# Second batch of a causal attention: tiles 8-9 by seven half-size products, tiles 6-7 with both scores in one step, and a new order of tiles and block loads

## The chip, the core and the metric

The kernel runs on one core of a Trainium2 chip. The engines named here are TensorE (PE, with its weight loads as PEld), VectorE (DVE), ScalarE (ACT), GpSimd (POOL) and the queue that SyncE feeds with transfers (SP). The metric is the device time of one launch in microseconds (us), the median of three runs.

## What is computed

The input x has 2 batches of 2048 tokens of 512 features. The part of the reference that matters here, shortened:

```python
xn = _layernorm(x)
q, k, v = x_norm @ qkv          # x_norm: xn normalised again
scores = einsum('bsk,btk->bst', q, k) * scale
scores = where(causal, scores, -inf)
attn = softmax(scores)
s = (attn @ v) @ o_proj + xn
g = silu(mixture_of_8_experts(xn, top 2))
return x + s * g
```

All of it is float32. The experts' result is stored in DRAM before the attention starts, and the attention gathers its rows back, two for each token.

## The kernel before

The attention is the last stage, about the last 400 us of the launch. It works on tiles of 128 queries, 16 in each batch, 32 in all; a list `seq` (L1014) gives their order. A place in that list is called a slot here: slots 0 to 15 are tiles 15 down to 0 of the first batch, slots 16 to 31 are tiles of the second batch. A causal tile t looks at keys 0 to 128(t+1)-1, in blocks of 512 keys; so tile 8 has two whole blocks and 128 keys more, tile 6 one block and 384 keys. Two slots that stand together share a query load and make a pair; pair 8 is slots 16 and 17, pair 9 is slots 18 and 19.

One long loop `for s in range(NT + OUT + 2)` (L1760) emits the program. In step s it emits scores of slot s, row maxima, exponentials, their transposition, and the product with the values of an earlier slot. Every engine works through its own instructions in exactly that order; nothing reorders them. The pieces, with the lines that the profile shows:

- Scores. `chunk_scores` (L1307 on PE) makes the scores of one slot against one key block with four matmuls into a PSUM bank. DVE masks the diagonal (L1312) and takes a maximum (L1295); `end_scores` joins the maxima to `nm` (L1395).
- Scores by seven products. For the pairs in `SCORED`, `fast_scores` makes the scores of both slots against the first two key blocks with seven products of half depth (L1359), 14 matmuls of 512 columns where the direct form takes 16. It needs sums of query parts, `query_sums` (L1326 to L1329, DVE, one step earlier), and sums of key parts, `block_sums` (L1340, the tile `tk`, one for each batch). ACT copies the first product out of PSUM (L1378), and DVE adds the others into place (L1365).
- Exponentials. `exponentials` runs on ACT (L1485). For slots with more than three tiles of keys POOL splits each result into halves (L1495), SP issues a transposing DMA (L1501), and DVE joins the halves again (`join_p`, L1517). Slots with up to three tiles of keys are turned by PE (L1512) and copied back by ACT (L1513).
- Values. `values` multiplies one slot directly (L1535, matmuls of 512 columns). For the pairs in `FAST` seven half-size products do it (L1583 and some of L1535, 256 columns each): `combine_p` makes sums of the two slots' probabilities (L1577, DVE), `combine_v` sums of the value blocks (L1557, tiles `vT`), and `values_first`, `values_next` and `values_end` make the products `p12`, `p57`, `p64` and `p03`. ACT copies a part of `p12` (L1611), and DVE adds up (L1600).
- Output. `gate` prepares the gathered rows (ACT L1688, DVE L1689, ACT L1691), `attended` scales the result (ACT L1696, DVE L1699), and `emit` finishes it on POOL (L1707, L1708). In an ordinary step, `attended` of an older slot comes on DVE ahead of the masks and maxima of the step.

[...] a pool "a" of five (scores, transposed tiles, products of the scores) and a pool "b" of three (products with values). Blocks of keys and values of the second batch are loaded during the first batch, by a table `parts_b` of steps; `later` is a table of the steps in which DVE makes `block_sums` and `combine_v` for the second batch. `joins` holds the `join_p` of the slot before.

Of the kernel before, what the change touches and what calls it, by code (L numbers as in the profile page):

```python
# [26 lines left out]
def gated_attention_moe(  # L27
# [32 lines left out]
    NT = B * S // P  # L60
    BT = 4
    TB = BT * P
    NB = NT // BT
    NBB = S // TB
# [928 lines left out]
    def fetch(store, pool, src, name, tag):  # L993

        def part(b, c):
            if c == 0:
                store[b] = pool().tile([P, src[b].shape[1], src[b].shape[2]], F32, name=f"{name}_{b}", tag=tag)
            nc.sync.dma_start(out=store[b][:, c, :], in_=src[b][:, c, :])
        return part
# [12 lines left out]

    assert B == 2 and NBB == 4
    seq = [t for t in reversed(range(NBB * BT))]  # L1014
    seq += [NBB * BT + t for t in (8, 9, 0, 1, 6, 7, 2, 3, 4, 5, 10, 11, 12, 13, 14, 15)]
    assert all(seq[s] // 2 == seq[s + 1] // 2 for s in range(0, NT, 2))
    fetch_k = fetch(aks, lambda: kp2, kt_d, "k2", "kT")
    fetch_v = fetch(avs, lambda: vp, v_d, "v2", "v")
# [249 lines left out]
    OUT = 4  # L1268


    SCORED = (0, 1, 2, 3, 13, 14, 15)
    FAST = SCORED + (4,)

    def place(s):
        b, t = divmod(seq[s], BT)
        return b, t, b - b % NBB
# [21 lines left out]
    def direct(s):  # L1298

        return range(2 if s // 2 in SCORED else 0, len(widths[s]))  # L1300

    def chunk_scores(s, j):
        b, t, first = place(s)
        w = widths[s][j]
        ps = ps_a.tile([P, TB], F32, name=f"ps_{s}_{j}", tag="a")
        for c in range(ND):
            nc.tensor.matmul(  # L1307
                ps[:, :w], lhsT=aqs[seq[s] // 2][:, c, ts(t % 2, P)], rhs=aks[first + j][:, c, :w],
                start=(c == 0), stop=(c == ND - 1),
            )  # L1310
        if first + j == b:
            nc.vector.tensor_tensor(ps[:, w - P : w], ps[:, w - P : w], keep, ALU.min)  # L1312
        maximum(s, ps[:, :w], j * TB)
# [79 lines left out]
    def end_scores(s):  # L1393
        mx, nm, pieces = scored[s]
        nc.vector.tensor_reduce(nm, mx[:, : len(pieces)], AX.X, ALU.max, negate=True)  # L1395
# [23 lines left out]
    for i in range(NM):  # L1419
# [21 lines left out]
        for _ in range(3):  # L1441
            if i >= paired.stop and early:
                f, b, c = early.pop(0)
# [249 lines left out]
    def attended(s):  # L1693
        n = seq[s]
        o = outs[s] if s // 2 in FAST else op.tile([P, D], F32, name=f"o_{s}", tag="o", bufs=4)
        nc.scalar.activation(  # L1696
# [34 lines left out]
    def emit_ahead(s, o, cols, attention=None):  # L1731
# [6 lines left out]

    K = NBB
    parts_b = [(0, fetch_v, 0), (0, fetch_v, 1), (0, fetch_v, 2), (0, fetch_v, 3),  # L1740
               (4, fetch_k, K + 2), (6, fetch_v, K + 2), (8, fetch_k, K + 1), (10, fetch_v, K + 1),
               (12, fetch_k, K), (14, fetch_v, K), (20, fetch_k, K + 3), (22, fetch_v, K + 3)]
    parts_b = [(s, f, b, c) for s, f, b in parts_b for c in range(ND)]
    parts_b.sort(key=lambda part: part[0])

    later = {}
    for steps, f, b in (
        ((10, 10, 11, 11), combine_v, K + 2), ((12, 12, 13, 13), combine_v, K + 1),
        ((20, 21, 22, 23), block_sums, K), ((24, 25, 26, 27), combine_v, K),
    ):  # L1750
        for i, step in enumerate(steps):
            later.setdefault(step, []).append((f, b, (i + 1,)))
# [6 lines left out]

    for s in range(NT + OUT + 2):  # L1760
        fast = s // 2 - 1 in FAST
        pair = (s, s + 1) if s // 2 in SCORED else (s,)
        if s < NT and (s % 2 == 0 or len(pair) == 1):
            for k in pair:
                if s:
                    begin_scores(k)
                room(k)
        n = s // 2 + 1
        if s % 2 == 0 and NQ <= n < NT // 2:
            for c in range(2):  # L1770
                fetch_q(n, c)
        if s == 0:
            fetch_parts(s, NBB * ND)
            block_sums(0)
        late = []
        for k in range(NT):
            if k not in AHEAD:
                wait = 4 - k % 2 if k // 2 in FAST else 3
                if s == k + wait:
                    late.append((attended, k))  # L1780
                if s == k + wait + 1:
                    emit(k)
        if s == NT:

            values_first(s - 2)
            for k in AHEAD:
                make_ahead(k)
        if len(pair) == 1 or s % 2:
            for f, *args in late:
                f(*args)  # L1790
        for k in range(NT):
            if s == (NT - 1 if k in AHEAD else k + 2 - k % 2 if k // 2 in FAST else k + 1):
                fetch_inputs(k)
        if s == NT - 1:
            gather_y(NT - 2)
        if s % 2 and s > 3 and s // 2 + 1 in SCORED:
            query_sums(s + 1, nc.vector)
        joins = []
        for k in () if s == 1 else (0, 1) if s == 2 else (s - 1,):
            if 0 <= k < NT - 1 and not by_te(k):  # L1800
                joins += [(join_p, k)] * len(halves[k])
        chunks = []
        if s < NT and s != 1:
            chunks = [(k, j) for k in ((1,) if s == 0 else (s,)) for j in direct(k)]
        if s == 0:

            for k, j in chunks:
                chunk_scores(k, j)
            chunks = []
        if s < NT and s % 2 == 0 and len(pair) == 2:  # L1810
            pools = [(ps_a, "a")] * 5 + [(ps_b, "b"), (ps_a, "a")]
            if s < 3:
                pools = [(ps_b, "b")] * 3 + [(ps_a, "a")]
            if s == 2:
                joins = [(combine_v, b, (1,)) for b in range(NBB - 1)] + joins
            now = 5 if s == 2 else 1
            fast_scores(s, pools, late + joins[:now])
            joins = joins[now:]
            if s == 0:
                query_sums(2, nc.gpsimd)  # L1820
        for k, j in chunks:
            chunk_scores(k, j)
            if s != 3 and joins:
                f, *args = joins.pop(0)
                f(*args)
        if s != 3:
            for f, *args in joins:
                f(*args)
        if 0 <= s - 1 < NT and by_te(s - 1):

            if not fast:
                values(s - 2)
            turn_p(s - 1)
        if s < NT and s != 1:
            end_scores(s)
        if fast and s % 2 == 0 and 2 < s < NT:
            combine_p(s - 2)
        if 0 <= s - 1 < NT:
            divisor(s - 1)
        if s < NT:  # L1840
            if s != 1:
                exponentials(s)
            if s % 2 == 0 and len(pair) == 2:
                maximum(s + 1, turned[s + 1][:, : 2 * TB], 0)
            if s == 0:
                end_scores(1)
                exponentials(1)
            fetch_parts(s, 4)
            for f, *args in later.pop(s, []):
                f(*args)  # L1850
        if s == 2:
            pass
        elif s == 3:
            combine_p(0, (1, 3, 2))
            for b in range(NBB - 1):
                combine_v(b, (2,))
            values_first(0)
            combine_p(0, (4,))
            for b in range(NBB - 1):
                combine_v(b, (4,))  # L1860
            values_next(0)
            for f, *args in joins:
                f(*args)
            values_end(0, [lambda: query_sums(s + 1, nc.vector)])
        elif s == NT:
            emit_ahead(s - 2, seven[s - 2][1], LO)
            values_next(s - 2)
        elif fast and s % 2 == 0:
            values_first(s - 2)

            if s != NT - 2:
                values_next(s - 2)
        elif fast and s == NT - 1:
            values_next(s - 3)
            values_end(
                s - 3,
                [lambda: join_p(s)] * len(halves[s])
                + [lambda: combine_p(s - 1, (1, 3)), lambda: gate(s - 1)]
                + [lambda: combine_p(s - 1, (2, 4))],
            )  # L1880
        elif fast:
            values_end(s - 3)
        elif 0 <= s - 2 < NT and not (s - 1 < NT and by_te(s - 1)):
            values(s - 2)

        for k in range(0, NT - 2, 2):
            if s == (k + 2 if k + 2 in AHEAD else k + 3):
                gate(k)
        for k in range(0, NT - 2, 2):
            if s == k + 1:  # L1890
                gather_y(k)
        if s == 1:

            for b in (2, 0, 1):
                combine_v(b, (3,), nc.gpsimd)
# [45 lines left out]
```

## Time and profile before

| | us |
|---|---|
| median of three runs (1007.63, 1008.37, 1008.95) | 1008.37 |
| the profiled execution | 1007.83 |
| its span, from first to last instruction | 1006.0 |
| PE busy, of the span | 999.9 |
| PEld busy | 665.3 |
| DVE busy | 716.9 |
| ACT busy | 403.2 |
| POOL busy | 483.3 |

The span and the profiled time differ by 1.8 us, which lies around the first and last instruction. The busy time of PE is that of matmuls whose records overlap each other; a float32 matmul of the program stands in the trace as two records, so a group of "x8" is four matmuls. Times in the timeline are counted from the start of the span. The stage between slots 16 and 20, which the change touches most, lies between 777 and 815 us in this execution.

### The profile page before, as it was taken

The numbers are of one execution on the slowest core, as the hardware profiler recorded it, in microseconds if no ns is written. First come the engines' busy times: TensorE is split into PE (matmuls) and PEld (weight loads), VectorE is DVE, ScalarE is ACT, GpSimd is POOL, SyncE is SP. The second block draws the span as 40 slices with busy tenths as digits, with TensorE's granted clock in tenths as the row PEclk, the third lists the DMA queues.
The fourth block names the chain that finished last, engine by engine and source line by source line (L and its number), as shares of the span: only waits on it lengthen the run. The fifth ranks groups of instructions, "written<-read, shape, count | busy, mean of one in ns | idle before, by whom it ended". The sixth has DMA issues, their size and how long they took to land. (4 is left out here: it accounts for less than half of the span.)

```text
span 1006.0 us, 13431 instructions
## 1 busy us (share of the span) xinstructions
PE 999.9 (99%) x3924; PEld 665.3 (66%) x3924; DVE 716.9 (71%) x1396; ACT 403.2 (40%) x804; POOL 483.3 (48%) x475
## 2 busy tenths in 40 slices
PE   9999999999999999999999999999999999999998
PEld 5888888874567767766753448677675544447577
DVE  6996746897887777677744579668576556878667
ACT  3344445322444454444445112232335535442241
POOL 4474564004644454444332165254557776764272
PEclk9999999999999999999999999999999999999999
DMA  8689996978999999999999576274677768753361
GB/s 293 193 264 293 329 286 258 349 249 240 202 227 220 211 208 221 217 200 222 216 218 242 164 193 147 78 206 104 183 199 239 225 200 240 207 141 86 92 165 42
DMA packets 296647, 207.96 MB, mean 207 GB/s; under 512 B 230776, under 2 KB 243832, under 8 KB 296576
## 3 DMA queue, kind: packets, MB, share of 16 engines
q1 hardware_dynamic: 282432, 163.56, 63.2%
q0 software_dynamic: 10400, 34.63, 12.5%
q10 hardware_dynamic: 3744, 8.91, 2.4%
q8 instruction: 34, 0.56, 0.2%
q14 instruction: 37, 0.30, 0.1%
HBM read 92.35 MB, written 60.03 MB: 151 GB/s over the span
## 5 line engine op out<-in xcount | busy, mean ns | idle before, releaser
L1195 PE MATMUL py<-arena,ht 128*128 (+3 forms) x396 | 176.7, 593 | 0.0
L1307 PE MATMUL ps<-k,q 128*128 128x512 f32 (+3 forms) x416 | 143.0, 495 | 0.3 <-PEq L1455 0.3
L1495 POOL COPY pu<-pT 128x1024 uint16<-128x1024 uint16 (+2 forms) x74 | 82.5, 1146 | 118.1 <-ACT pT L1485 59.1
L1166 POOL COPY hu<-h 128x704 uint16<-128x704 uint16 x66 | 61.9, 956 | 155.8 <-issue 121.7
L1195 PEld LDWEIGHTS py<-arena,ht 128*128 128x128 f32 (+3 forms) x396 | 71.8, 185 | 80.7 <-issue 76.9
L1307 PEld LDWEIGHTS ps<-k,q 128*128 128x128 f32 x416 | 74.7, 190 | 67.1 <-issue 56.5
L970 POOL DMA_INDIRECT xs<-zu_d,toki x66 | 77.6, 1176 | 70.2 <-DVE toki L791 55.6
L1181 ACT ACTIVATE ht<-ht,b1sel 128x128 f32<-128x128 f32 (+3 forms) x216 | 67.9, 380 | 88.1 <-DVE ht L1175 88.1
L1145 DVE TENSOR_TENSOR h<-p,h 128x176 f32<-128x176 f32 x182 | 55.5, 337 | 60.7 <-PE p L1138 57.2
L1678 POOL DMA_INDIRECT yg<-y_d,posi x64 | 67.4, 1053 | 36.9 <-DVE yg L1689 21.9
L1535 PE MATMUL po<-v,pT 128*128 128x512 f32 x152 | 67.9, 592 | 0.0
L347 POOL COPY zu<-z 128x1024 uint16<-128x1024 uint16 x32 | 39.9, 1245 | 55.7 <-DVE z L332 55.7
L1517 DVE COPY pT<-puT 128x1024 uint16<-128x1024 uint16 (+2 forms) x74 | 54.1, 759 | 8.8 <-DMA puT<-pu 8.6
L1485 ACT ACTIVATE pT<-pT,nm 128x1024 f32<-128x1024 f32 x14 | 16.1, 1148 | 110.3 <-DVE nm L1395 72.0
L1203 ACT COPY y<-py 128x512 f32<-128x512 f32 x55 | 32.2, 585 | 62.3 <-PE py L1195 48.4
L1485 ACT ACTIVATE pT<-ps,nm 128x512 f32<-128x512 f32 (+3 forms) x52 | 30.1, 581 | 62.5 <-DVE nm L1395 38.8
L1365 DVE TENSOR_TENSOR pT<-p,pT 128x512 f32<-128x512 f32 x49 | 32.9, 687 | 25.8 <-PE p L1359 22.1
L1535 PEld LDWEIGHTS po<-v,pT 128*128 128x128 f32 x152 | 28.6, 190 | 31.9 <-issue 30.1
L1707 POOL TENSOR_TENSOR o<-o,yg 128x512 f32<-128x512 f32 x30 | 42.0, 1398 | 14.3 <-DVE o L1699 14.1
L1699 DVE SCALAR_TENSOR_TENSOR o<-xo,xscale,o 128x512 f32<-128x512 f32 x30 | 25.9, 871 | 30.1 <-ACT o L1696 30.1
L1046 DVE COPY xT<-xhT 128x1024 uint16<-128x1024 uint16 x66 | 45.2, 712 | 2.3 <-DMA xhT<-xs 2.0
L1708 POOL TENSOR_TENSOR o<-o,xo 128x512 f32<-128x512 f32 x30 | 43.0, 1432 | 2.4
(342 smaller groups left out, 2142.9 us busy)
## 6 DMA issues: line engine op xcount, KB each, us to landing
y_d<-y SPq DMA_DIRECT2D x66, 256.0 KB, 4.4
zu_d<-zu SPq DMA_DIRECT2D x32, 264.0 KB, 2.8
kt_d<-kT SPq DMA_DIRECT2D x16, 512.0 KB, 5.9
q<-qt_d SPq DMA_DIRECT2D x32, 256.0 KB, 5.4
k<-kt_d SPq DMA_DIRECT2D x32, 256.0 KB, 4.7
v<-v_d SPq DMA_DIRECT2D x32, 256.0 KB, 5.6
xo<-in_x_dram SPq DMA_DIRECT2D x32, 256.0 KB, 3.8
x<-in_x_dram SPq DMA_DIRECT2D x30, 256.0 KB, 4.9
```

The source lines that it names most:

```text
L970: nc.gpsimd.indirect_dma_start(out=xs, out_offset=None, in_=zu_d, in_offset=bass.IndirectOffsetOnAxis(ap=toki[:, order[i] : order[i] + 1], ...
L1046: nc.vector.tensor_copy(xT.bitcast(U16).rearrange("p c (t h) -> p c t h", h=2), xhs.pop(i).rearrange("p (h c) t -> p c t h", h=2),)
L1145: nc.vector.tensor_tensor(out, x, y, ALU.add)
L1166: nc.gpsimd.tensor_copy(hu[:, :, :H], h.bitcast(U16).rearrange("p (d h) -> p h d", h=2))
L1181: nc.scalar.activation(ht[:hn, c, at], ht[:hn, c, at], AF.Silu, bias=b1sel[:hn, c, j : j + 1])
L1195: nc.tensor.matmul(py[at, :], lhsT=ht[:k, c, at], rhs=rhs[n], start=(c == 0), stop=(c == NH - 1),)
L1307: nc.tensor.matmul(ps[:, :w], lhsT=aqs[seq[s] // 2][:, c, ts(t % 2, P)], rhs=aks[first + j][:, c, :w], start=(c == 0), stop=(c == ND - 1),)
L1485: nc.scalar.activation(turned[s][:, at:end], src, AF.Exp, bias=nm, accum_out=rs[:, j : j + 1])
L1495: nc.gpsimd.tensor_copy(pu[:, : 2 * w].rearrange("p (h d) -> p h d", h=2), turned[s][:, k : k + w].bitcast(U16).rearrange("p (d h) -> p h ...
L1517: nc.vector.tensor_copy(turned[s][:, k : k + w].bitcast(U16).rearrange("p (i t h) -> p i t h", t=P, h=2), puT[:, : 2 * w // P, :].rearrang ...
L1535: nc.tensor.matmul(dst, lhsT=turned[s][:, ts(k, P)], rhs=avs[first + k // BT][:, k % BT, cols], start=(start and k == k0), stop=(k == k1 - 1),
L1678: nc.gpsimd.indirect_dma_start(out=y, out_offset=None, in_=y_d, in_offset=bass.IndirectOffsetOnAxis(ap=posi[k][:, n : n + 1], axis=0),)
```

## The change

Four things change in the emitting loop and its tables; no function that computes is altered.

1. The order of the second batch becomes 8, 9, 6, 7, 0, 1, 2, 3, 4, 5, 10 and so on. It was 8, 9, 0, 1, 6, 7, 2, 3, 4, 5, 10.
2. Pair 8 (tiles 8 and 9) joins `SCORED` and with it `FAST`: its scores against key blocks 0 and 1 of the batch and its values are made by seven products.
3. The block loads come in the order 1, 0, 2 instead of 2, 1, 0, at the same steps. `block_sums` of the second batch moves from steps 20 to 23 to steps 10 to 13. `combine_v` of block 0 moves from steps 24 to 27 to steps 14 and 15, that of block 2 from steps 10 and 11 to steps 20 to 23.
4. A new set `JOINT` holds pair 9 (tiles 6 and 7). In its even step (18) the loop emits: the older slot's `attended`, the scores of tile 6, the `join_p` of slot 17, `combine_p` of pair 8, the end of tile 6's maxima and its exponentials, then the scores, maxima and exponentials of tile 7. The products of pair 8 with the values follow, and step 19 makes no scores. In the step before (17), the rest of tile 9's scores, the end of its maxima and its exponentials are emitted ahead of the `join_p` of slot 16.

```diff
-    seq += [NBB * BT + t for t in (8, 9, 0, 1, 6, 7, 2, 3, 4, 5, 10, 11, 12, 13, 14, 15)]
+    seq += [NBB * BT + t for t in (8, 9, 6, 7, 0, 1, 2, 3, 4, 5, 10, 11, 12, 13, 14, 15)]
...
-    SCORED = (0, 1, 2, 3, 13, 14, 15)
+    SCORED = (0, 1, 2, 3, 8, 13, 14, 15)
     FAST = SCORED + (4,)
+    JOINT = (9,)
...
-               (4, fetch_k, K + 2), (6, fetch_v, K + 2), (8, fetch_k, K + 1), (10, fetch_v, K + 1),
-               (12, fetch_k, K), (14, fetch_v, K), (20, fetch_k, K + 3), (22, fetch_v, K + 3)]
+               (4, fetch_k, K + 1), (6, fetch_v, K + 1), (8, fetch_k, K), (10, fetch_v, K),
+               (12, fetch_k, K + 2), (14, fetch_v, K + 2), (20, fetch_k, K + 3), (22, fetch_v, K + 3)]
...
-        ((10, 10, 11, 11), combine_v, K + 2), ((12, 12, 13, 13), combine_v, K + 1),
-        ((20, 21, 22, 23), block_sums, K), ((24, 25, 26, 27), combine_v, K),
+        ((10, 11, 12, 13), block_sums, K), ((12, 12, 13, 13), combine_v, K + 1),
+        ((14, 14, 15, 15), combine_v, K), ((20, 21, 22, 23), combine_v, K + 2),
...
-        pair = (s, s + 1) if s // 2 in SCORED else (s,)
+        joint = s < NT and s // 2 in JOINT
+        pair = (s, s + 1) if s // 2 in SCORED or joint else (s,)
...
-            chunks = [(k, j) for k in ((1,) if s == 0 else (s,)) for j in direct(k)]
+            here = () if joint else (1,) if s == 0 else (s,)
+            chunks = [(k, j) for k in here for j in direct(k)]
+        if (s + 1) // 2 in JOINT and s % 2:
+            for k, j in chunks:
+                chunk_scores(k, j)
+            end_scores(s)
+            exponentials(s)
+            chunks = []
...
+        if joint and s % 2 == 0:
+            for f, *args in late:
+                f(*args)
+            for j in direct(s):
+                chunk_scores(s, j)
+            for f, *args in joins:
+                f(*args)
+            joins = []
+            if fast:
+                combine_p(s - 2)
+            end_scores(s)
+            exponentials(s)
+            for j in direct(s + 1):
+                chunk_scores(s + 1, j)
+            end_scores(s + 1)
+            exponentials(s + 1)
...
-        if s < NT and s != 1:
+        begun = joint or s % 2 and (s + 1) // 2 in JOINT
+        if s < NT and s != 1 and not begun:
             end_scores(s)
-        if fast and s % 2 == 0 and 2 < s < NT:
+        if fast and s % 2 == 0 and 2 < s < NT and not joint:
             combine_p(s - 2)
```

More of the change, by code (lines that the diff above doesn't have):

```diff
@@ L1809, in gated_attention_moe @@
             chunks = []
-        if s < NT and s % 2 == 0 and len(pair) == 2:
+        if joint and s % 2 == 0:
[14 more added lines that the diff above has]
+            exponentials(s + 1)
+        if s < NT and s % 2 == 0 and s // 2 in SCORED:
             pools = [(ps_a, "a")] * 5 + [(ps_b, "b"), (ps_a, "a")]
@@ L1840, in gated_attention_moe @@
         if s < NT:
-            if s != 1:
+            if s != 1 and not begun:
                 exponentials(s)
-            if s % 2 == 0 and len(pair) == 2:
+            if s % 2 == 0 and s // 2 in SCORED:
                 maximum(s + 1, turned[s + 1][:, : 2 * TB], 0)
```

## Prediction

> **What bounds the kernel now.** First the page: shares by engine, the granted clock, the chain that ended last.
>
> ```profile
> PE 999.9 (99%) x3924; PEld 665.3 (66%) x3924; DVE 716.9 (71%) x1396; ACT 403.2 (40%) x804; POOL 483.3 (48%) x475
> ...
> PEclk9999999999999999999999999999999999999999
> ...
> PE 43%; DVE 1%; issue 0%
> ```
>
> The clock is full in every slice and the chain is nearly all PE. A busy PE need not be one at its peak, so next come the waits of PE from 600 us to the end, then the PE timeline:
>
> ```profile
> PE p L1583 <- DVE u L1600: 0.4, 1, 0.4
> ```
>
> ```profile
> 709.95 3.62 PE L1583 MATMUL p<-v,pT 128*128 128x256 f32 x16
> 713.41 1.03 PE L1535 MATMUL p<-v,pT 128*128 128x256 f32 x4
> ...
> 773.42 1.06 PE L1307 MATMUL ps<-k,q 128*128 128x128 f32 x8
> 774.32 2.74 PE L1535 MATMUL po<-v,pT 128*128 128x512 f32 x6
> ...
> 797.05 7.89 PE L1535 MATMUL po<-v,pT 128*128 128x512 f32 x18
> 804.77 1.89 PE L1307 MATMUL ps<-k,q 128*128 128x256 f32 x8
> ```
>
> One wait of 0.4 us in 400: PE runs without a gap. Start to start, 18 records of 512 columns take 7.72 us, 0.429 each, and 16 of 256 take 3.46 us, 0.216 each. With two records to a matmul that is **0.858 us and 0.432 us**. PE's sum sets the time, and everything else is worth what it makes PE wait.
>
> **What PE saves.** Scores of pair 8 against two blocks: 16 matmuls become 14, 2 x 0.858 = 1.72 us. Values: direct, 9 + 10 key tiles, 19 x 0.858 = 16.30 us. By seven products over 8 key tiles, 7 x 4 = 28 half-width matmuls, and 2 + 4 for the keys left over: 34 x 0.432 = 14.69 us. Saved: 1.61 us. Together **3.3 us**; the built order of the two kernels shows just these counts. Moving slots 18 to 21 and reordering the loads keeps PE's sum. Everything below can only give some of it back.
>
> **Loads and SP.** The three key blocks keep their steps and sizes, each needed at slot 16 or later; the issues of steps 8 and 12 stand at 718 and 764 us, long before 777. The query load of pair 9 stays at step 16 and SP passes no more transfers than before: the two puT pairs of step 18 simply stand together. I cost all this at nothing; if the cover were gone it would be one landing, 4.7 us for keys by the page.
>
> **DVE, steps 10 to 13 (A).** `block_sums` takes the place of two `combine_v` parts in steps 10 and 11 and is added in 12 and 13. In step 12 DVE afterwards waits for a transfer until 765.96 anyway, which hides it. In step 13 it delays what follows:
>
> ```profile
> 769.75 1.40 DVE L1689 SCALAR_TENSOR_TENSOR yg<-yg,share,yg 128x512 f32<-128x512 f32 x2
> ```
>
> ```profile
> 771.19 1.06 ACT L1691 ACTIVATE yg<-yg 128x1024 f32<-128x1024 f32 x1 [0.28 <-DVE yg L1689]
> 772.15 0.76 ACT L1696 ACTIVATE o<-po,xshift,ri 128x512 f32<-128x512 f32 x1
> 773.68 0.48 ACT L1513 COPY pT<-pt 128x384 f32<-128x384 f32 x1 [0.77 <-PE pt L1512]
> ```
>
> A tk part of this form took 1.20 us at 832.48. Then L1689, L1691 and L1696 move by 1.2, L1696 ends at 774.1, and the copy L1513, which PE's product at 774.32 needs, ends at 774.55 instead of 774.16. The slack was 0.16, so PE waits **0.25 us** (0 to 0.5: another tk part took 1.44).
>
> **Query sums (B).** They are new in step 15, behind `combine_v` and L1699, so they begin near 778.3, while PE begins the first product at 777.4 and needs the second sum four matmuls later, at 780.8. What a sum costs depends on POOL:
>
> ```profile
> 888.58 1.49 DVE L1328 TENSOR_TENSOR sq<-q 128x256 f32<-128x256 f32 x1
> 889.99 0.41 DVE L1329 TENSOR_TENSOR sq<-q,sq 128x256 f32<-128x256 f32 x1
> ```
>
> 0.41 alone, up to 1.49 beside POOL: ready between 779.1 and 781.3. Behind the sums wait slot 15's mask, its exponential on ACT, the gate (L1688 to L1691), and the copy of the first product (L1378), at about 787.5; the seventh product takes that bank at 787.9. B is 0 to 1.4; the earlier sums at 861 to 866 end near the middle, and I take **0.2 us**.
>
> **Steps 16 to 19 (C).** This is the part that no row shows as a whole. PE, put together by the counts above, starts tile 6's scores near 794.9, tile 7's at 800.9, p12 at 807.8, p57 at 811.6, p64 at 815.1, p03 at 816.8, and the second half of p64 at 819.8. DVE has: the joins of slot 16, the gate of slot 14, L1699, tile 6's maxima, the joins of slot 17, four `combine_p`, tile 7's maxima, and only then the addition that frees p12's bank for p03 (its three "b" banks are p12, p57, p64). Rows:
>
> ```profile
> 788.48 0.69 ACT L1485 ACTIVATE pT<-ps,nm 128x512 f32<-128x512 f32 x1
> ```
>
> ```profile
> 793.69 1.57 DVE L1517 COPY pT<-puT 128x1024 uint16<-128x1024 uint16 x1 [1.21 <-DMA puT<-pu]
> ...
> 912.03 0.82 DVE L1577 TENSOR_TENSOR pT<-pT,pT 128x640 f32<-128x640 f32 x1
> 912.77 1.66 DVE L1577 TENSOR_TENSOR s<-s,pT 128x640 f32<-128x640 f32 x1
> ```
>
> From an exponential to its first join are 5.2 us. Slot 16's exponential starts near 794.7, so its three joins end near 802.3; gate and L1699 (ACT between them) end at 806.7; maxima 1.4, joins 1.6, four sums of 512 elements 4 x 0.65: slot 18's nm at 812.3. Tile 7's maxima 1.7, its exponentials 1.5, the copy L1611 and the addition 0.8: p12's bank is free at 816.3, 0.5 before p03 wants it. The joins of slot 18 (5.2 us and a second transfer 1.3 after nm) and the first u addition end near 820.1, 0.3 late for p64. So C is 0.3 with no POOL beside the sums. POOL's L1707 and L1708 of slot 14 stand just there (1.27 and 1.26 us in its rows): with two of the four sums beside them at the dear price, 0.8 more each by the two L1577 rows, p03 waits 1.1 and p64 another 0.6. Ends 0.3 and 1.7; nearest are the mixed rows, and I take **1.0 us**.
>
> [...]
>
> **Steps 20 to 25.** Four small tiles now stand together and PE's steps 22 and 23 hold 3.6 and 5.3 us. The tightest is slot 22's exponential, about 1 us before PE turns it: nothing, or some tenths. The `combine_v` moved away from steps 24 to 27 was hidden behind a gapless PE and gains nothing.
>
> **Sum.** -3.3 + 0.25 + 0.2 + 1.0 = -1.9 us on the execution's own 1007.83: 1005.9. The median stands 0.5 above that execution; so **1006.5 us**.
>
> **Rivals.**
> 1. All of the saving stays: POOL and DVE miss each other, A to C are below 0.6. 1007.83 - 3.0 + 0.5 = 1005.3. For it: one wait in 400 us now. Against it: three slacks below 0.5 us. Chance 0.13.
> 2. Given back whole: A 0.5, B 1.2, C 1.7 make 3.4 us, 1008.4. For it: the dear rows above. Chance 0.14.
> 3. Slower: the DVE chain of step 18 ends PE's wait. If every join and every sum there meets POOL (joins 1.57 instead of 0.68[...]), nm of slot 18 comes 4.8 to 6.5 us later, and p03 with p64 wait about 5.5 us: -3.3 + 0.45 + 5.5 = +2.7, 1011.0. It decides once C passes 2.9 us. [...] Today's longest wait is 0.43 us and the clock row shows only nines, so by the row nothing is added[...]. Against it: in the sequence 911 to 916 only two of four sums were dear. Chance 0.20.
> 4. That the change doesn't do what it says is excluded by the built order.
>
> **How the numbers follow.** A measurement of this kernel can't tell less than 0.2%, 2.0 us, from no change. The forecast, 0.53, lies on that bound: half of it on each side. Faster: 0.13 + 0.26 = 0.39. Within: 0.27 + 0.07 = 0.34. Slower: 0.20 + 0.07 from the second rival's far side = 0.27. The likeliest case alone spans 1005.3 to 1008.0. The range takes in the whole saving at the low end and most of the slower case: 1004.8 to 1010.6.
>
> **What would show it.** The saving: 34 more matmuls of 256 columns and, net, 21 fewer of 512 in the second batch, with the same start-to-start times. A: a wait of the product at about 774.5 for ACT L1513. B: the third product waiting for DVE sq, or the seventh for ACT. C: waits of L1583 or L1535 for DVE o or u near 817 to 821. Wrong would be the whole if PE had one wait above 3 us there, if it waited in the small tiles of steps 20 to 25, or if the clock row showed less than nines.

## The result, and the profile after

The changed kernel is slower: **1016.9 us** (median of 6 runs, 1014.7 to 1020.3) against 1008.4 before (1007.6 to 1009.0), a ratio of **1.0086** (95% interval 1.0066 to 1.0106). The profiled execution took 1018.42 with a span of 1016.7, 10.7 above the span before; in the other runs the mean granted clock was 0.994 to 0.998 and the time went with it, so the median shows less of the loss (8.5 us) than the trace does.

First the page again: the busy time of each engine, the clock in 40 slices, and the chain that ended last.

```profile
PE 1002.0 (99%) x3950; PEld 672.1 (66%) x3950; DVE 736.3 (72%) x1417; ACT 403.5 (40%) x802; POOL 481.7 (47%) x475
...
PEclk9999999999999999999999999999999999899999
...
PE 30%; POOL 6%; issue 5%; DMA 2%; DVE 1%; ACT 0%; SPq 0%; POOLq 0%; DVEq 0%; ACTq 0%
```

PE is busy 2 us longer, though it has less work: one slice of the clock row has an eight. The chain now leaves PE and runs over POOL, SP and DMA. The waits of PE from 600 us to the end (total, times, longest) say where:

```profile
PE po L1536 <- DVE pT L1518: 3.4, 1, 3.4
PE p L1584 <- DVE s L1578: 2.9, 1, 2.9
PE p L1360 <- DVE sq L1328: 1.8, 1, 1.8
```

Below these stand only the old wait of 0.4 and one of 0.3. (Line numbers of the changed kernel are one larger than in the old profile.) In order of time, from the PE timeline:

```profile
774.88 2.84 PE L1536 MATMUL po<-v,pT 128*128 128x512 f32 x6 [0.34 <-issue]
...
783.17 5.42 PE L1360 MATMUL p<-tk,sq 128*128 128x512 f32 x12 [1.80 <-DVE sq L1328]
...
817.04 3.41 PE L1584 MATMUL p<-vT,s 128*128 128x256 f32 x8 [2.94 <-DVE s L1578]
...
869.99 6.37 PE L1536 MATMUL po<-v,pT 128*128 128x512 f32 x8 [3.43 <-DVE pT L1518]
```

Four new waits; I call them A and B, as in the prediction, **S** (for the first `combine_p` sum of slots 16 and 17) and **V** (the values of slot 23). Start to start each costs some 0.15 more than the bracket says, because the record of the matmul ahead reaches past the start of the next (eight records of 512 columns take 3.60 us, the row behind them starts 3.43 after they do). And the last two carry something else: eight records of 256 columns take 1.89 us elsewhere and 3.41 here, eight of 512 take 3.60 and here 6.37. The stretches (length, busy time of PE, PEld, DVE, ACT and POOL, then the granted clock, the share of the DMA engines and GB/s) show why:

```profile
813.00:817.00 4.00, 1.10 (x6) 0.62 (x4) 3.97 (x5) 0.00 (x0) 2.33 (x2) 1.00 0.83 301
817.00:820.30 3.30, 3.26 (x9) 2.64 (x10) 3.23 (x7) 1.25 (x4) 0.41 (x1) 0.56 0.56 169
866.00:870.00 4.00, 0.57 (x4) 0.20 (x2) 0.85 (x2) 0.00 (x0) 1.26 (x1) 0.83 0.95 223
870.00:873.20 3.20, 3.20 (x4) 1.47 (x5) 1.49 (x6) 1.80 (x5) 1.75 (x3) 0.50 0.93 344
873.20:876.20 3.00, 3.00 (x6) 1.15 (x4) 2.97 (x4) 0.00 (x0) 2.62 (x2) 0.63 0.56 109
```

After each of the two long waits PE runs at about half clock: for some 3 us after S and for more than 5 us after V, where the clock has fallen before the wait is over (0.83 in that stretch). The first product of the next pair, before and after:

```profile
865.59 3.60 PE L1359 MATMUL p<-k,q 128*128 128x512 f32 x8
...
876.20 3.60 PE L1360 MATMUL p<-k,q 128*128 128x512 f32 x8
```

The 10.6 us between are -3.3 of saving, +0.5 (A), +2.0 (B), +3.1 and 1.5 of slow clock (S), +3.6 and 2.8 of slow clock (V), and some tenths.

**Why S waits.** The DVE timeline, joins of slot 16, joins of slot 17, first sum:

```profile
802.69 4.09 DVE L1518 COPY pT<-puT 128x1024 uint16<-128x1024 uint16 x3 [0.93 <-DMA puT<-pu]
...
812.31 3.99 DVE L1518 COPY pT<-puT 128x1024 uint16<-128x1024 uint16 x3
816.22 0.68 DVE L1578 TENSOR_TENSOR s<-pT 128x512 f32<-128x512 f32 x1
```

By the cheap rows the first three joins make 0.68 + 0.68 + 0.28, the second three 0.68 + 0.68 + 0.43. They took 4.09 and 3.99. Beside the first three POOL makes its output sums (L1708, L1709) of slot 13, from 801.13 to 803.7, and copies `pu` until 807.2; beside the second three it makes the output sums of slot 14:

```profile
812.46 1.27 POOL L1708 TENSOR_TENSOR o<-o,yg 128x512 f32<-128x512 f32 x1
813.81 1.60 POOL L1709 TENSOR_TENSOR o<-o,xo 128x512 f32<-128x512 f32 x1
```

The four sums themselves, which I had feared for, took the cheap 0.68 or 0.69 each.

**Why V waits.** SP's queue, and the join of slot 23 on DVE:

```profile
855.88 1.87 SPq L998 DMA_DIRECT2D v<-v_d  x4
858.02 0.34 SPq L1710 DMA_DIRECT2D out_dram<-o  x1
858.46 0.38 SPq L1667 DMA_DIRECT2D xo<-in_x_dram  x1
859.47 1.38 SPq L1502 DMA_TRANSPOSE puT<-pu  x1
...
869.15 0.69 DVE L1518 COPY pT<-puT 128x1024 uint16<-128x1024 uint16 x1 [5.36 <-DMA puT<-pu]
```

The load of the last value block (1 MB) goes out 3.6 us ahead of the transposition of slot 23, whose join starts only at 869.15, 9.7 us after the issue. Before, this load went out 7.3 us ahead of that transposition, whose join did not wait:

```profile
845.37 1.86 SPq L998 DMA_DIRECT2D v<-v_d  x4
...
852.63 1.24 SPq L1501 DMA_TRANSPOSE puT<-pu  x1
```

In the changed kernel SP was held until 855.00 by output stores of small tiles, which wait for POOL (SP's waits from 835 to 870 us; the longest single one is 11.8):

```profile
SPq L1710 <- POOL o L1709: 23.4, 5, 11.8
```

### The profile page after: what moved, and what is told of

Read it like the earlier page. It is cut to its first block, busy times and chain, and to the rows that moved or that the text cites. A ratio compares the mean times of both kernels' runs of the same rounds, so it can differ in the third digit from the quotient of the medians.

```text
span 1016.7 us, 13501 instructions
## 1 busy us (share of the span) xinstructions
PE 1002.0 (99%) x3950; PEld 672.1 (66%) x3950; DVE 736.3 (72%) x1417; ACT 403.5 (40%) x802; POOL 481.7 (47%) x475
## 5 line engine op out<-in xcount | busy, mean ns | idle before, releaser
L1308 PE MATMUL ps<-k,q 128*128 128x512 f32 (+3 forms) x384 | 129.1, 486 | 0.3 <-PEq L1456 0.3
L1308 PEld LDWEIGHTS ps<-k,q 128*128 128x128 f32 x384 | 68.6, 190 | 59.3 <-issue 47.6
L1518 DVE COPY pT<-puT 128x1024 uint16<-128x1024 uint16 (+2 forms) x74 | 58.3, 820 | 12.4 <-DMA puT<-pu 12.4
L1486 ACT ACTIVATE pT<-pT,nm 128x1024 f32<-128x1024 f32 x16 | 18.4, 1148 | 113.5 <-DVE nm L1396 75.3
L1536 PE MATMUL po<-v,pT 128*128 128x512 f32 x114 | 54.1, 620 | 3.8 <-DVE pT L1518 3.4
L1366 DVE TENSOR_TENSOR pT<-p,pT 128x512 f32<-128x512 f32 x56 | 37.5, 687 | 27.8 <-PE p L1360 18.6
L1486 ACT ACTIVATE pT<-ps,nm 128x512 f32<-128x512 f32 (+3 forms) x48 | 27.3, 572 | 62.9 <-DVE nm L1396 38.3
L1708 POOL TENSOR_TENSOR o<-o,yg 128x512 f32<-128x512 f32 x30 | 42.3, 1410 | 14.7 <-DVE o L1700 14.6
L1584 PE MATMUL p<-vT,s 128*128 128x256 f32 x180 | 43.3, 389 | 2.9 <-DVE s L1578 2.9
L1360 PE MATMUL p<-tk,sq 128*128 128x512 f32 x96 | 42.6, 593 | 1.8 <-DVE sq L1328 1.8
L1709 POOL TENSOR_TENSOR o<-o,xo 128x512 f32<-128x512 f32 x30 | 42.7, 1423 | 2.4
```

The lines of the kernel that those rows point to most:

```text
L1308: nc.tensor.matmul(ps[:, :w], lhsT=aqs[seq[s] // 2][:, c, ts(t % 2, P)], rhs=aks[first + j][:, c, :w], start=(c == 0), stop=(c == ND - 1),)
L1360: nc.tensor.matmul(ps, lhsT=x[:, c], rhs=y[:, c], start=(c == 0), stop=(c == ND // 2 - 1))
L1518: nc.vector.tensor_copy(turned[s][:, k : k + w].bitcast(U16).rearrange("p (i t h) -> p i t h", t=P, h=2), puT[:, : 2 * w // P, :].rearrang ...
L1536: nc.tensor.matmul(dst, lhsT=turned[s][:, ts(k, P)], rhs=avs[first + k // BT][:, k % BT, cols], start=(start and k == k0), stop=(k == k1 - 1),
L1584: nc.tensor.matmul(dst, lhsT=a[:, k], rhs=v(k), start=(k == 0), stop=(stop and k == n - 1))
L1708: nc.gpsimd.tensor_tensor(o, o, g, ALU.mult)
```

## The experiments

All are edits of the changed kernel unless said otherwise; times are medians, ratios are against the kernel before on the same chip.

**First round: one wait at a time.** e1 moves the load of value block 7:

```diff
-               (12, fetch_k, K + 2), (14, fetch_v, K + 2), (20, fetch_k, K + 3), (22, fetch_v, K + 3)]
+               (12, fetch_k, K + 2), (14, fetch_v, K + 2), (20, fetch_k, K + 3), (24, fetch_v, K + 3)]
```

> The load of value block 7 is issued in step 24 instead of step 22; nothing else is changed. If the transposition of slot 23 was late because it stood behind this 1 MB load: it lands within 3.5 us of its issue again, TensorE's wait of 3.4 us at the values of slot 23 is gone, and with it the half clock after it; 3.6 + 2.8 = 6.4 us less, 1010.5. If the order of the tiles alone, the gathers or the output stores made it late: the join still waits over 8 us on its transfer and the time stays within 1 us of 1016.9. If the load only moves the collision: a wait of 2 us or more on a join of slots 24 or 25, and 1013 or more.

1012.99, ratio 1.0045 (1.0035 to 1.0055). V and the slow clock behind it are gone, the other waits are as they were (2.9 and 1.8). The size, 3.9 us, is short of 6.4, since the profiled execution had more than its share of V: four of the six runs of the changed kernel show a clock of 0.997 or 0.998, against 0.994 there.

e2 moves `combine_v` of block 4 behind the query sums:

```diff
-        ((14, 14, 15, 15), combine_v, K), ((20, 21, 22, 23), combine_v, K + 2),
+        ((15, 15, 16, 16), combine_v, K), ((20, 21, 22, 23), combine_v, K + 2),
```

> The subtractions of value block 4 (combine_v) run in steps 15, 15, 16, 16 instead of 14, 14, 15, 15, so that two of them no longer stand between the maxima of slot 15 and the query sums of step 15. If the third product waited because the sums stood behind these two (1.64 us each beside GpSimd): TensorE's wait at line 1360 falls from 1.8 to under 0.4 us, and the time falls by 1.6 to 1015.3. If the slow DVE beside GpSimd is the cause wherever the rows stand: the wait stays over 1 us and the time within 1 us of 1016.9. The other two waits (2.9 and 3.4 us) stay in both.

1017.70, ratio 1.0082 (1.0054 to 1.0110). B falls from 1.8 to 0.7, but not under 0.4, S grows from 2.9 to 3.7: no gain.

e3 takes the joins of slot 17 and the four sums ahead in step 18:

```diff
         if joint and s % 2 == 0:
-            for f, *args in late:
-                f(*args)
-            for j in direct(s):
-                chunk_scores(s, j)
             for f, *args in joins:
                 f(*args)
...
             if fast:
                 combine_p(s - 2)
+            for f, *args in late:
+                f(*args)
+            for j in direct(s):
+                chunk_scores(s, j)
```

> In step 18 the joins of slot 17 and the four sums of slots 16 and 17 run ahead of the emission of slot 14 and of the maxima of slot 18. If the order on DVE made the first sum late: it ends by 813 us instead of 816.9, TensorE's wait of 2.9 us at line 1584 falls to under 0.6, the stretch behind it runs at full clock (1.5 us), and the time falls by some 4.3 to 1012.6. If the slow joins beside GpSimd or the transpositions' landing decide: the first sum still ends after 815, the wait stays over 1.5 us, and the time falls by less than 2. A new wait at the exponentials of slot 18, which now follow, would give the gain back at its values in step 20.

1018.14, ratio 1.0090 (1.0062 to 1.0118). S shrinks from 2.9 to 0.7, and the longest waits of PE show what took its place:

```profile
PE p L1536 <- DVE o L1601: 3.7, 1, 3.7
PE po L1536 <- DVE pT L1518: 2.4, 1, 2.4
```

The maxima of slots 18 and 19 came later, ACT made their exponentials later, and the copy L1612 of the first value product, which stands behind them in ACT's queue (at 823.48), held the output sum that PE's p03 waits for. e4 puts the three edits together:

> The three edits together. If the three waits are separate and the halved clock goes with them: 6.4 + 1.6 + 4.3 = 12.3 us less, 1004.6, which is under the kernel before (1008.4), near the predicted saving of 3.3; mean clock 0.999 or more. If the waits stand for one shortage of DVE, and clearing one lengthens another: 1008 or more.

1015.03, ratio 1.0064 (1.0045 to 1.0082). V is gone and B is at 0.7, but S is back at 3.5: the third transposition of slot 17 landed at 813.1 and its join met slot 14's sums on POOL (1.49 instead of 0.43). So far only V was cured by its own edit; of the waits on DVE, one shrinks and another grows.

**Second round: parts of the change, and POOL.** e5 is the kernel before with the new order of tiles alone; e11 is e5 with the load in step 24 as in e1.

```diff
-    seq += [NBB * BT + t for t in (8, 9, 0, 1, 6, 7, 2, 3, 4, 5, 10, 11, 12, 13, 14, 15)]
+    seq += [NBB * BT + t for t in (8, 9, 6, 7, 0, 1, 2, 3, 4, 5, 10, 11, 12, 13, 14, 15)]
```

> The kernel before with the new order of the tiles alone (8, 9, 6, 7, 0, 1, 2, ...): no seven products for tiles 8 and 9, no joint step, loads and sums as before. If the order alone bunches the small tiles so that the load of value block 7 goes out late and the transposition of slot 23 stands behind it: TensorE waits 2 us or more at the values of slot 23, half clock after it, 1012 or more. If the lateness needs the new steps ahead of it as well: no wait over 0.5 us in the small tiles and 1008.4 within 1 us.

1011.78, ratio 1.0038 (1.0026 to 1.0051). The longest waits of PE in e5, with the old line numbers:

```profile
PE po L1535 <- DVE pT L1517: 2.5, 1, 2.5
PE p L1359 <- ACT pT L1485: 1.0, 1, 1.0
```

**The wait V comes from the order alone**, with no seven products for tiles 8 and 9 and no joint step.

> e5 (the kernel before with the new order of tiles alone) with the load of value block 7 in step 24. If that load is all that the order costs: the wait of 2.5 us at the values of slot 23 goes, and with it the 1.0 us at the scores behind it; 1011.8 - 3.4 = 1008.4, the same as before. If the order costs something else: 1010 or more.

1010.29, ratio 1.0023 (1.0012 to 1.0035): V is gone, but the wait for ACT's exponential of slot 25 has grown to 1.6. DVE ends slot 25's maxima at 871.8, before at 867.9: it is behind through all the small tiles, and, as before the change, the query sums of slots 26 and 27 (three of the four took 1.25 to 1.49 us, against 0.41 for a cheap one) stand ahead of them. So the order costs more than the load.

e6 is e1 with `JOINT = ()`: tiles 6 and 7 scored in separate steps.

> After with the load of block 7 in step 24, and without the joint step: tiles 6 and 7 are scored in steps 18 and 19, one in each, so that TensorE has one tile's scores (6.5 us) less ahead of the values of slots 16 and 17. If the joint step is what covers the joins, and 2.9 us of it were still missing: the wait at line 1584 grows from 2.9 to some 8 us, and the time from 1013.0 to 1018 or more. If the joint step itself made the sums late: the wait gets shorter, and the time falls to 1010 or less.

1022.41, ratio 1.0144 (1.0127 to 1.0161). S is 10.4 us long. The joint step is no cause of S; it hides 7.5 us of this chain, and not quite all of it.

e8 is e1 with POOL's output sums of slot 14 one step later:

```diff
-                if s == k + wait + 1:
+                if s == k + wait + 1 + (k == 14):
```

> After with the load of block 7 in step 24, and the output sums of slot 14 on GpSimd (line 1708 and 1709) in step 19 instead of step 18; DVE's order is unchanged. If GpSimd beside the joins made them dear: the joins of slot 17 take 0.7, 0.7 and 0.4 us instead of 2.0, 1.8 and 0.4, the first sum ends near 814.8, the wait at line 1584 falls from 2.9 to about 0.9, its half clock goes, and the time falls from 1013.0 to 1009.5. If the joins wait for the transpositions or are dear by themselves: the wait stays over 2 us and the time within 1 us of 1013.0.

1011.42, ratio 1.0032 (1.0021 to 1.0044). DVE, in the order it had:

```profile
812.47 1.62 DVE L1518 COPY pT<-puT 128x1024 uint16<-128x1024 uint16 x3
814.01 0.69 DVE L1578 TENSOR_TENSOR s<-pT 128x512 f32<-128x512 f32 x1
```

The three joins of slot 17 take 1.62 us instead of 3.99, S falls from 2.9 to 0.6, and its slow clock is gone; the joins of slot 16 still take 4.05 and do not bring S back. The median moved by only 1.6 of the 3.5 expected (by 1.3 in the ratios, since e1 and e8 ran on different chips); two waits of 0.6 and 0.7 at line 1601's output sums appeared behind it.

e7 had the load and POOL edits of e8, the query sums ahead of the emission in step 15, and in step 18 the maxima and exponentials of slot 18 first, with the emission between the joins:

> The load of block 7 in step 24; the query sums of slots 16 and 17 ahead of the emission in step 15; the output sums of slot 14 on GpSimd one step later, away from the joins of slot 17; and in step 18 on DVE: maxima of slot 18, joins of slot 17 with the emission between them, two sums, maxima of slot 19, two sums. If the waits come from what stands ahead of the sums on DVE and beside them on GpSimd: the waits at lines 1360 and 1584 fall under 0.6 each with no new one over 1 us, clock 0.999 or more, and 1013.0 - 1.8 - 2.9 - 1.5 = 1006.8. If the transpositions' landing (812.5) or ScalarE's queue decide: a wait of over 1.5 us stays, 1009 or more.

1012.12, ratio 1.0039 (1.0025 to 1.0053): a miss. With the exponentials ahead of it in ACT's queue, L1697 came at 811.87 instead of 809.61 as in e8; the emission L1700 on DVE waited for it, then took 2.20 beside POOL's `pu` copy, and the second join behind it started at 814.79. S was 3.3 again.

**Third round: all waits out.** e9 is e8 with the query sums of slots 16 and 17 at the end of step 14, and step 18 in this order: maxima of slot 18, two joins, emission, third join, two sums, maxima of slot 19, two sums. e10 adds `block_sums` in steps 10, 10, 11, 12.

> As e8 (load of block 7 in step 24, output sums of slot 14 one step later), and the query sums of slots 16 and 17 at the end of step 14, ahead of the subtractions of block 4; in step 18 on DVE: maxima of slot 18, two joins of slot 17, the emission, the third join, two sums, exponentials' maxima of 18 and 19, two sums. If the waits come from DVE's order: line 1360's 1.8 us goes (2.0 us with its refill), the three of 0.6 to 0.7 at the values of slots 16 and 17 fall to under 0.3 each, and 1011.4 - 2.0 - 1.7 = 1007.7. If the rows only change places and the sums then meet GpSimd elsewhere: waits of 2 us in sum stay, 1009.5 or more.

> As e9, with the four differences of key block 4 in steps 10, 10, 11, 12 instead of 10, 11, 12, 13, so that none stands ahead of the emission in step 13. If this is the 0.34 us wait at line 1536 near 775 (0.5 with its refill): it goes, 0.5 less than e9. If the differences only delay another row on DVE: no gain, or a new wait before 770.

1009.63 (1.0021, 1.0012 to 1.0029) and 1009.23 (1.0011, 1.0000 to 1.0023). B and S are gone; e9 fell short of 1007.7, for a wait of 0.9 for `u` (L1601, which stands behind the joins of slot 18) and one of 1.0 for slot 25's exponential are left. e10 took A away, and a `tk` difference of 1.97 us in step 11 then doubled the old wait of 0.43 at 751.

e13 uses steps 10, 10, 12, 12 and puts the joins of slot 18 behind the output sums of L1601:

> As e10, with the four differences of key block 4 in steps 10, 10, 12, 12, and in step 19 the joins of slot 18 behind the output sums of slots 16 and 17 (line 1601) instead of ahead of them. If the last waits come from DVE's order: the 1.0 us at line 1584 near 823 goes (1.2 with its refill), and the 0.95 near 752 falls back to 0.4; 1009.2 - 1.2 - 0.5 = 1007.5, and the kernel beats the one before (1008.1) by what is left of the saving of 3.3. If the joins of slot 18 are then late for the values of slot 18: a wait of over 0.5 us at 826, and no gain.

1008.09, ratio 1.0000 (0.9993 to 1.0007): the `u` wait is gone, 0.9 at the values of slot 19 and 1.0 at slot 25's exponential stay. e14 goes after these two as well:

```diff
+            if s in (14, 24):
+                query_sums(s + 2, nc.vector)
             for f, *args in later.pop(s, []):
...
+        if s == 20:
+            for f, *args in joins + late:
+                f(*args)
+            joins = []
```

> As e13, with the query sums of slots 26 and 27 at the end of step 24 and the joins of slot 19 ahead of the emission in step 20. If DVE's order made the last two waits (0.91 us at line 1536 near 833, 1.04 at line 1360 near 871; 2.3 with their refills): they go, and 1008.1 - 2.3 = 1005.8, faster than the kernel before. If GpSimd beside the moved rows makes them dear at their new place: 1007.5 or more.

**1006.19, ratio 0.9985 (0.9978 to 0.9993)**: under both kernels. Against the one before it is 2.1 us by the medians and 1.5 by the ratio, less than the 0.2% that the prediction takes as the least to be told from no change, though the interval stays below 1. All that PE waits for after 600 us in e14:

```profile
PE p L1360 <- ACT pT L1486: 0.7, 2, 0.4
PE p L1360 <- ACT pT L1379: 0.4, 1, 0.4
```

**Fourth round: each cause put back alone into e14.**

> e14 with the load of value block 7 back in step 22. If that load alone makes the transposition of slot 23 late, whatever the rest: a wait of 2.4 to 3.4 us at the values of slot 23 and nothing else; e14 + 2.6 if the clock stays, e14 + 6 if a wait of 3 us halves it (so 1008.4 to 1012). If the earlier order of DVE brought slot 23's transposition ahead of the load: within 0.5 of e14.

1011.94, ratio 1.0036 (1.0022 to 1.0050), 5.8 us over e14. The transposition is issued at 856.80 and joined at 865.91, 9.1 us (in e14 at 853.41 and 857.66, 4.3 us, with no wait). The join in e15 and in e14, then PE in e15:

```profile
865.91 0.69 DVE L1518 COPY pT<-puT 128x1024 uint16<-128x1024 uint16 x1 [4.78 <-DMA puT<-pu]
...
857.66 0.69 DVE L1518 COPY pT<-puT 128x1024 uint16<-128x1024 uint16 x1
```

```profile
866.75 5.37 PE L1536 MATMUL po<-v,pT 128*128 128x512 f32 x8 [2.84 <-DVE pT L1518]
```

2.84 of wait, 0.15 for the overlap, and 1.8 more than 3.60 for the eight records: 4.8 of the 5.8. The rest is not traced; the five runs of e15 lie 3.5 us apart.

> e14 with the output sums of slot 14 on GpSimd back in step 18, beside the joins and sums of slots 16 and 17. If GpSimd beside DVE is the price, whatever DVE's order: the third join and the first sum take 1.5 to 2.2 us each instead of 0.4 and 0.7, a wait of 1.5 to 3 us at line 1584, e14 + 1.6 to 5. If DVE's order was the price and GpSimd's place does not matter in the new order: within 0.5 of e14.

1010.80, ratio 1.0021 (1.0012 to 1.0030), 4.6 us over e14. DVE's third join and first sum in e16, POOL's two operations, and then PE:

```profile
811.86 2.17 DVE L1518 COPY pT<-puT 128x512 uint16<-128x512 uint16 x1 [0.25 <-issue]
813.95 1.75 DVE L1578 TENSOR_TENSOR s<-pT 128x512 f32<-128x512 f32 x1
...
812.46 1.27 POOL L1708 TENSOR_TENSOR o<-o,yg 128x512 f32<-128x512 f32 x1
813.81 1.33 POOL L1709 TENSOR_TENSOR o<-o,xo 128x512 f32<-128x512 f32 x1
```

```profile
815.84 3.65 PE L1584 MATMUL p<-vT,s 128*128 128x256 f32 x8 [2.75 <-DVE s L1578]
```

In e14 the two DVE rows take 0.43 and 0.68. The two operations of POOL lengthen a join and a sum, PE waits 2.75 us, and its eight records then take 3.65 instead of 1.89: 0.15 + 2.75 + 1.76 = 4.7.

> e14 with the query sums of slots 16 and 17 back in step 15, behind the subtractions of block 4 and the emission. If that order is what the third product waited for: 1.8 us at line 1360 again, e14 + 1.5 (2.0, less the waits of 0.35 and 0.36 at 784 and 788 that the early sums brought). If the earlier differences of block 4 had already cured it: within 0.5 of e14.

1006.91, ratio 0.9988 (0.9981 to 0.9995), only 0.7 over e14: B is back with 1.8 us, but the two waits of 0.4 at 784 and 788, which the early sums had brought, are gone in exchange.

## Why the prediction was wrong

- **The saving** of 3.3 us was right. From 773 to the next pair's first product, e8 is 2.3 us longer than before, and its waits with their refills in that stretch make 5.6. In e14, where nearly all waits are gone, 1.5 to 2.1 us of it are left.
- **A** (0.25, range 0 to 0.5): 0.5, the upper end. The `tk` part took 1.97 us, not 1.20.
- **B** (0.2, range 0 to 1.4): 2.0. The place was right, the third product waiting for `sq`. Mis-sized was the start of the sums, "near 778.3": it was 781.19, because the two `combine_v` rows and L1699 ahead of them were priced at their cheap time and took 1.64, 1.64 and 1.75 beside POOL (cheap rows: 0.68, 0.68, 0.75). I let POOL slow only the sums.
- **C** (1.0, range 0.3 to 1.7): 3.1 of wait, 4.6 with the clock. The term that failed is the joins. "Its three joins end near 802.3" and "joins 1.6" took the cheap rows; they cost 4.09 and 3.99. I had reserved the dear price for the four sums, which were cheap in the changed kernel. Of the two groups it is the joins of slot 17 that PE waits for: in e8 and e14 those of slot 16 still take over 4 us. So the first sum, not the additions behind it, came too late, and p57 waited; p03 and p64 did not, in the changed kernel. In e8, with POOL's 1.27 and 1.60 us away, the three joins are 2.4 us shorter. I let POOL slow the sums and passed over the copies.
- **The third rival** had the mechanism (dear joins, C above 2.9) and put it at the additions of step 19; S alone, 3.1 us of wait and 4.6 with the clock, is what it priced at 5.5. That was an estimate, and the rows of the old trace give as much: three joins at 0.89 more and four sums at 0.84 more (1.66 for 0.82) are 6.0 us, less the 0.5 by which p12's bank is free ahead of p03. I gave it 0.20, because only two of four *sums* had been dear in the old trace; the join of 1.57 us quoted above it, with POOL's L1708 beside it until 794.71, was the row to go by.
- **Steps 20 to 25** ("nothing, or some tenths") failed outright, and with it the "nothing" for loads and SP: V is 3.6 us of wait and 2.8 of slow clock, the largest single loss in the trace. I followed the loads of steps 4 to 14, which the change renames, and not the load of step 22, which it doesn't touch: the new order moves the small tiles, whose output stores hold SP's queue for POOL, and so the load goes out 10.5 us later, while the transposition moves by 6.8, and only 3.6 us are left between them. e5 has it from the order alone; e1 and e15 switch it off and on.
- **The clock** was not in the sum. The third rival went by today's longest wait, 0.43 us, and the row of nines ("by the row nothing is added"), and they hold nothing on a wait of 2 us or more. The waits of 2.9 and 3.4 us cost 4.3 us more; recorded waits of 2.75 to 2.94 (e16, e15, S) were enough for half clock.
- "What would show it" named three signs for a wholly wrong prediction: a wait above 3 us, waits in the small tiles, less than nines in the clock row. All three came.

What stays open: how the load makes the transposition of slot 23 late, by its place in the queue or by the bandwidth it takes, and whether the POOL gathers, which run beside that transposition, have a share in its 9 us. They run there in e14 too, where it takes at most 4.3; they were not moved apart from the load.

## What to carry to other kernels

A reordering is not priced by the instructions that it moves: follow also the untouched transfers in a queue that waits for another engine, because their issue moves with that wait (here a 1 MB load, by 10.5 us). Where DVE is the engine that PE waits for next, price every copy and two-input row beside GpSimd at its dear row (here 2.17 us for 0.43, 1.75 for 0.68), and move GpSimd's work a step away before reordering DVE: e8 did with one condition what e3 could not do with DVE's order, and e7, with the same condition and a new order on DVE, lost it again. When waits trade places, clear them all once, then put the causes back one by one.

## What the hardware showed

- **Half clock after a short wait.** Waits of 2.42 us (e3) and 2.46 us (e5) were followed by eight records in 3.67 us, full speed. After 2.75 (e16), 2.84 (e15), 2.94 and 3.43 us (after), the following eight took 1.5 to 2.8 us too long. After 3.33 (e7), 3.52 (e4), 3.72 (e3) and 10.36 us (e6) the next eight of 256 columns took 3.00, 3.01, 3.53 and 3.75 us instead of 1.89; in e1 (2.9) and e2 (3.7 and 3.0) the execution's mean clock was 0.998 and 0.995. These runs give no sharp bound: in e16 four of twelve runs had a mean clock of 1.000, three of them at 1008.3 to 1008.5, the other eight 0.997 or 0.998 at 1010.2 to 1012.6; in e5 two of six runs had 0.998. Nor did the clock fall at a fixed time. At S it fell 0.4 us after the wait had ended, 3.3 us after PE's last record. In V (first row) it fell with PE still waiting, some 2 us after PE's last record; in e3, whose wait of 3.72 was longer, it was full up to the end of the wait at 824.36 (second row) and fell only about 1 us later:

```profile
868.00:869.00 1.00, 0.00 (x0) 0.00 (x0) 0.00 (x0) 0.00 (x0) 0.00 (x0) 0.80 1.09 327
...
823.60:824.36 0.76, 0.00 (x1) 0.00 (x1) 0.42 (x1) 0.76 (x3) 0.42 (x1) 1.00 1.11 213
```

- **How long it lasted.** In slices of 0.25 us of the changed kernel, 815 to 822.5 and 866 to 877, the clock is 1.00 or 0.50 in all but four, the ones in which it changes (0.81 and 0.87, 0.70 and 0.64). A slice of 1 us with a clock of 0.80 is counted as 0.4 us at half clock on that account. Summed in this way the half clock lasted 3.4 us at S and 6.8 us, twice as long, at V. In e3, e4, e7, e15 and e16 the records behind the wait took 1.8 us too long together, as they did behind S; by that it was some 3.4 us there too, an estimate.
- **A DVE row beside POOL ended just after one of POOL's.** The 128x512 join took 0.43 us in e14 and 2.17 beside POOL in e16; the 128x1024 one 0.68 without POOL and 1.5 to 2.0 beside it. In e16 the join's record ends 0.30 us after POOL's first operation has ended, and the sum's 0.56 after the second: less than the 0.43 and 0.68 that they take alone. In the changed kernel the first two joins of slot 17 end 0.56 and 0.55 us after L1708 and L1709. POOL pays as well: its `pu` copy of 1024 columns took 1.03 us ahead of the joins of slot 16 and 1.50 beside them.
- **A transposing transfer behind a 1 MB load.** From issue to join it took 9.7 us (after) and 9.1 us (e15) with the load 3.6 us ahead, 7.1 us (e5) with it 4.1 ahead, and at most 4.4 us with it 7.3 ahead (before) or without it (e14).
